# Token routing laid out as 784 consecutive tokens on each partition, with the zero fill and the second layer's weights placed elsewhere

## The chip, the core and the metric

The kernel runs on one core of one Trainium2 chip. Its engines are TensorE (PE, with PEld for its weight loads), VectorE (DVE), ScalarE (ACT) and GpSimd (POOL); SyncE (SP) issues most of the DMAs. Each engine takes its instructions in order and waits for the others on semaphores. The metric is the device time of one execution in microseconds. The time before is 16481.53 us, the median of three runs (16472.82 to 16503.21).

## What is computed

Two layers over x of shape 32 x 128 x 56 x 56, that is T = 100352 tokens of C = 128 channels. The first is a 7x7 depthwise convolution, a layer norm and a mixture of E = 8 experts with two picks for each token and a limit on each expert's tokens; the second is a convolution block with a Mamba scan over each image. The routing of the first layer is what matters here:

```python
logits = xf @ Wg + bg
topv, topi = jax.lax.top_k(logits, 2)
wts = jax.nn.softmax(topv, axis=-1)
order = jnp.argsort(-wts[:, 0])              # surest tokens first
cap = int(1.25 * T / E)                      # 15680 places for each expert
pos = cumsum(one_hot(topi[order]))           # place among the tokens of that expert
keep = pos < cap
buf[slot] = xf[order]                        # one row for each kept pick
y = gelu(buf @ W1 + b1) @ W2 + b2            # by expert
moe = sum over the two picks of y[slot] * weight
out = input + xf + layer_scale * moe
```

An expert that more tokens pick than it has places for keeps those of highest weight; where weights are equal, the earlier token goes first.

## The kernel before

The program is written as stages, one after the other. A scheduler gives each engine its order; it keeps close to the program's order, but it may take an instruction forward if its operands and its memory are ready. Memory is handed out in pools: the tiles of a closed pool make room for those of the next, and an instruction that writes into reused memory waits. Before the change a pool waits for all the tiles of the pool that lay there.

1. **Convolution** (L113 to L269). Images are taken in batches of four. `fill` loads an image into the single tile `xt` (L145), turns it on PE and copies it into `xc`. `conv` multiplies by Toeplitz tiles; in batch 0 these come from the raw taps (`raw`, L162, from `taps_d`, which the prologue makes from seven tap loads, L138, and one store, L139) and are kept in `toep_d`; later batches load them (L172). `norm` (16 for a batch) does the layer norm of seven columns of tokens, stores them to `res_d` (L213; `xa` has three buffers) and makes the logits; `top2` leaves the two picks and the difference of their logits in `picks` and `less`. The work of `norm` and `top2` for a batch is laid between the convolutions of the next, and for the last batch it follows the last convolution.
2. **Zero fill** (L272 to L274). The places of the experts' buffer `buf_d`, 125440 rows of 520 bytes, are written with zeros and the index T, from a constant tile of 112 rows, row by row, in 14 DMAs on SP. The tile is made at the start (L67 to L69), and the DMAs stand on SP's queue from 3.1 us on, among those of the convolution.
3. **Routing** (L277 to L442). Tokens lie as in the convolution, 112 on the partitions and 896 columns. `key` holds for each expert its tokens' weights. A search of 24 steps (L354 to L358) halves the interval for each expert's threshold: `count` counts the tokens over the bound (four experts on ACT with Sign, four on DVE), `totals` adds over the partitions on PE, and two small DVE instructions move the bounds of all eight experts. Then for each expert the places: masks of those over and at the threshold, on PE the counts of tokens before them, a scan over the columns, and the sums `sl`. At the end the places and the weights are turned on PE to 128 partitions (L431 to L442), giving `slots` and `gates`.
4. **Scatter** (L451 to L473). Blocks of 128 x 28 tokens are loaded to `xg` (L465, three buffers for each pick), and 1568 indirect DMAs on POOL (L469) write 128 rows each to their places.
5. **Experts** (L478 to L564). Blocks of 512 rows are loaded (`xb`, L552), turned and multiplied on PE, and added to `res_d` by 984 indirect DMAs on POOL (L518).
6. **Layer 1's weights** (L567 to L709). 28 loads on SP, among them six small columns that the scheduler takes forward into the routing, then some small work that makes `wk`, `wz`, `wo` and others from them.
7. **Layer 1** (L714 on). An order written by hand, `work`, over 224 chunks of 448 tokens. `fetch` loads `x1` and `yg` (the latter from `res_d`, L762), `moe_pe` (L770 to L772) adds them up on PE.

The DMAs of SP start in the order of its queue, and an issue is held up when what is ahead has not drained; the zero fill, the raw taps, `xt`, `toep`, `res_d`, `xg`, `xb` and the weights all use it.

Of the kernel before, what the change touches and what calls it, by code (L numbers as in the profile page):

```python
# [5 lines left out]
F32 = mybir.dt.float32  # L6
# [16 lines left out]
KF = FF // 128  # L23
GT = 4
# [19 lines left out]
def tile_kernel(tc: tile.TileContext, a: dict, out: bass.AP):  # L44
# [6 lines left out]
    QB = COLS // 128  # L51
    assert CAP % TT == 0
# [4 lines left out]
    with (  # L57
# [8 lines left out]

        zero = const.tile([TT, 1, RW], F32, name="zero")  # L67
        nc.gpsimd.memset(zero, 0.0)
        nc.gpsimd.memset(zero[:, :, C + 1].bitcast(I32), T)  # L69
# [26 lines left out]
        routed = tc.tile_pool(name="route", bufs=1)  # L96
# [175 lines left out]
        buf_t = buf_d[: E * CAP].rearrange("(k p) c -> p k c", p=TT)  # L272
        for k in range(0, E * CAP // TT, 80):
            nc.sync.dma_start(out=buf_t[:, k : k + 80, :], in_=zero.to_broadcast([TT, 80, RW]))  # L274


        with (  # L277
            tc.tile_pool(name="rt", bufs=1) as rt,
            tc.tile_pool(name="rs", bufs=2) as rs,
            tc.tile_pool(name="rp", bufs=2, space=PSUM) as rp,  # L280
        ):
            ones_tt = rt.tile([TT, TT], F32, name="ones_tt")
            nc.vector.memset(ones_tt, 1.0)
            before = rt.tile([TT, TT], F32, name="before")
            nc.gpsimd.affine_select(
                out=before, in_=ones_tt, compare_op=ALU.is_gt, fill=0.0, base=0,
                pattern=[[1, TT]], channel_multiplier=-1,
            )
            pb = rp.tile([TT, TT], F32, name="p_before", tag="tot")
            nc.tensor.matmul(pb, lhsT=before, rhs=perm, start=True, stop=True)  # L290
            half = rt.tile([TT, TT], F32, name="half")
            nc.vector.tensor_copy(half, pb)
            pb = rp.tile([TT, TT], F32, name="p_before", tag="tot")
            nc.tensor.matmul(pb, lhsT=half, rhs=perm, start=True, stop=True)
            nc.vector.tensor_copy(before, pb)
            ones_row = rt.tile([TT, COLS], F32, name="ones_row")
            nc.vector.memset(ones_row, 1.0)

            slots = [route.tile([128, QB, TT], I32, name=f"slot{k}") for k in range(2)]
            gates = [route.tile([128, QB, TT], F32, name=f"gate{k}") for k in range(2)]  # L300
            key = rt.tile([TT, E, COLS], F32, name="key")
            m = rt.tile([TT, COLS], F32, name="m")

            w0 = rt.tile([TT, COLS], F32, name="w0")
            w1 = rt.tile([TT, COLS], F32, name="w1")
            nc.scalar.activation(w1, less, AF.Exp)
            nc.vector.tensor_scalar_add(w0, w1, 1.0)
            nc.vector.reciprocal(w0, w0)
            nc.vector.tensor_tensor(w1, w1, w0, ALU.mult)

            nc.vector.tensor_scalar_max(m, w0, 0.5)
            for e in range(E):
                second = rs.tile([TT, COLS], F32, name="second")
                for k, t in enumerate((key[:, e, :], second)):
                    nc.vector.scalar_tensor_tensor(t, picks[k], float(E - e), m, ALU.is_equal, ALU.mult)
                nc.vector.scalar_tensor_tensor(key[:, e, :], key[:, e, :], -0.5, second, ALU.add, ALU.add)

            cnt = rt.tile([TT, E], F32, name="cnt")

            def totals():  # L320

                p = rp.tile([TT, E], F32, name="p_tot", tag="tot")
                nc.tensor.matmul(p, lhsT=ones_tt, rhs=cnt, start=True, stop=True)
                return p
# [4 lines left out]
            EV = E // 2  # L329
            thr = rt.tile([TT, E], F32, name="thr")  # L330
            cand = rt.tile([TT, E], F32, name="cand")
            odd = rt.tile([TT, E], F32, name="odd")
            step = rt.tile([TT, E], F32, name="step")
            need = rt.tile([TT, E], F32, name="need")
            nc.vector.memset(need[:, :EV], float(CAP))
            nc.vector.memset(need[:, EV:], float(2 * CAP - T))
            nc.vector.memset(thr, 0.0)

            def count(lim, op, shift):

                nc.vector.tensor_scalar(odd[:, EV:], lim[:, EV:], -(2.0**25), shift, ALU.mult, ALU.add)
                for e in range(EV, E):
                    sign = rs.tile([TT, COLS], F32, name="sign")
                    nc.scalar.activation(
                        sign, key[:, e, :], AF.Sign, bias=odd[:, e : e + 1], scale=2.0**25,
                        accum_out=cnt[:, e : e + 1],
                    )
                for e in range(EV):
                    junk = rs.tile([TT, COLS], F32, name="junk")
                    nc.vector.tensor_scalar(  # L350
                        junk, key[:, e, :], lim[:, e : e + 1], None, op, ALU.add, accum_out=cnt[:, e : e + 1]
                    )

            for b in range(1, 25):  # L354
                nc.vector.tensor_scalar_add(cand, thr, 2.0**-b)
                count(cand, ALU.is_ge, 1.0)
                nc.vector.tensor_tensor(step, totals(), need, ALU.is_ge)
                nc.vector.scalar_tensor_tensor(thr, step, 2.0**-b, thr, ALU.mult, ALU.add)  # L358


            count(thr, ALU.is_gt, -1.0)
            room = rt.tile([TT, E], F32, name="room")
            p = totals()
            nc.vector.tensor_scalar(room[:, :EV], p[:, :EV], -1.0, float(CAP), ALU.mult, ALU.add)
            nc.vector.tensor_scalar(room[:, EV:], p[:, EV:], -0.5, float(CAP - T // 2), ALU.mult, ALU.add)

            PB = min(448, COLS)
            NB = COLS // PB
            assert NB * PB == COLS and NB <= 2

            tots = [[rt.tile([TT, 1 + COLS], F32, name=f"tot{k}_{i}") for i in range(2)] for k in range(2)]
            for k in range(2):
                for i in range(2):
                    nc.vector.memset(tots[k][i][:, 0:1], 0.0)
            masks = [dict() for e in range(E)]

            def mask(e):

                for k, op in enumerate((ALU.is_gt, ALU.is_equal)):
                    t = masks[e][k] = rs.tile([TT, COLS], F32, name=f"mask{k}")
                    nc.vector.tensor_scalar(t, key[:, e, :], thr[:, e : e + 1], None, op)
                    pin = masks[e]["in", k] = rp.tile([TT, NB, 512], F32, name=f"p_in{k}", bufs=1)
                    pall = rp.tile([TT, NB, 512], F32, name="p_all", bufs=1)
                    for j in range(NB):
                        mj = t[:, j * PB : (j + 1) * PB]
                        nc.tensor.matmul(pall[:, j, :PB], lhsT=ones_tt, rhs=mj, start=True, stop=True)
                        nc.tensor.matmul(pin[:, j, :PB], lhsT=before, rhs=mj, start=True, stop=True)
                    nc.scalar.copy(  # L390
                        tots[k][e % 2][:, 1:].rearrange("p (j t) -> p j t", j=NB), pall[:, :, :PB]
                    )


            sl = [rt.tile([TT, COLS], F32, name=f"sl{k}") for k in range(2)]
            for k in range(2):
                nc.vector.memset(sl[k], 0.0)
            mask(0)
            for e in range(E):
                if e + 1 < E:  # L400
                    mask(e + 1)
                gt, eq = masks[e][0], masks[e][1]
                rk = []
                for k in range(2):
                    r = rs.tile([TT, COLS], F32, name=f"rk{k}")
                    nc.vector.tensor_tensor_scan(r, ones_row, tots[k][e % 2][:, :COLS], 0.0, ALU.mult, ALU.add)
                    rv = r.rearrange("p (j t) -> p j t", j=NB)
                    nc.vector.tensor_tensor(rv, masks[e]["in", k][:, :, :PB], rv, ALU.add)
                    rk.append(r)

                lim = room[:, e : e + 1]
                nc.vector.scalar_tensor_tensor(eq, rk[1], lim, eq, ALU.is_lt, ALU.mult)
                nc.vector.tensor_tensor(gt, gt, eq, ALU.add)
                nc.vector.scalar_tensor_tensor(rk[0], rk[1], lim, rk[0], ALU.min, ALU.add)
# [5 lines left out]
            for k in range(2):  # L420
                nc.vector.tensor_scalar_add(sl[k], sl[k], float(ZR))
            for k, w in enumerate((w0, w1)):
                nc.vector.scalar_tensor_tensor(w, sl[k], float(ZR), w, ALU.is_lt, ALU.mult)
# [784 lines left out]
```

## Time and profile before

| what | value |
|---|---|
| median of the runs | 16481.53 us |
| the profiled execution | 16440.87 us, span 16439.1 us |
| convolution, last logits | to 1664.94 us |
| routing, first indirect DMA of the scatter | to 2002.13 us |
| scatter, first load for the experts | to 3999.20 us |
| experts, last issue of an indirect DMA | to 5926.99 us |
| layer 1 | from there to the end |
| granted TensorE clock, mean | 0.905 |

The profile is of one execution. Times are from the span's start. Its page gives each engine's busy time, its share in 40 slices (a slice is 411 us, a digit is tenths), the groups of instructions and their releasers, and the DMA queues. A timeline row has the start, the length, the engine, the line in the code, the operation, what it writes and reads, and in brackets how long the engine stood before it and what ended that. A row of a queue (SPq) has the time that the issue took, not the transfer's.

### The profile page before, as it was taken

The numbers are of one execution on the slowest core, as the hardware profiler recorded it, in microseconds if no ns is written. First come the engines' busy times: TensorE is split into PE (matmuls) and PEld (weight loads), VectorE is DVE, ScalarE is ACT, GpSimd is POOL, SyncE is SP. The second block draws the span as 40 slices with busy tenths as digits, with TensorE's granted clock in tenths as the row PEclk, the third lists the DMA queues.
The fourth block names the chain that finished last, engine by engine and source line by source line (L and its number), as shares of the span: only waits on it lengthen the run. The fifth ranks groups of instructions, "written<-read, shape, count | busy, mean of one in ns | idle before, by whom it ended". The sixth has DMA issues, their size and how long they took to land. (4 is left out here: it accounts for less than half of the span.)

```text
span 16439.1 us, 246023 instructions
## 1 busy us (share of the span) xinstructions
PE 12744.6 (78%) x91548; PEld 6997.7 (43%) x91548; DVE 11159.9 (68%) x9974; ACT 10663.7 (65%) x20955; POOL 13614.8 (83%) x9017
## 2 busy tenths in 40 slices
PE   5997200002999989998898999999989899989998
PEld 4997100001777744444444444444444444444443
DVE  1564700000111149999999999999999999999999
ACT  3555300001444458888888888888888888888887
POOL 1434177777888879999999999999999999999999
PEclk8997555556999999999999999999999999999999
DMA  9879233333555545555555555555555555555555
GB/s 257 237 231 230 67 102 106 102 106 76 71 70 72 70 103 175 175 174 176 174 176 174 175 175 176 173 175 177 174 174 173 175 176 174 174 177 175 173 176 162
DMA packets 1360754, 2572.09 MB, mean 156 GB/s; under 512 B 139112, under 2 KB 801856, under 8 KB 1355456
## 3 DMA queue, kind: packets, MB, share of 16 engines
q1 hardware_dynamic: 1163072, 2361.89, 47.6%
q0 software_dynamic: 196480, 194.45, 6.9%
q8 instruction: 721, 11.81, 0.3%
q14 instruction: 481, 3.94, 0.1%
HBM read 2180.38 MB, written 375.43 MB: 155 GB/s over the span
## 5 line engine op out<-in xcount | busy, mean ns | idle before, releaser
L1053 POOL TENSOR_TENSOR db<-du,bb 128x896 f32<-128x896 f32 x3584 | 6856.5, 1938 | 17.6
L1059 ACT ACTIVATE da<-dt,aneg 128x449 f32<-128x449 f32 x7168 | 4577.8, 639 | 269.2 <-DVE prod L1074 86.5
L1068 DVE TENSOR_TENSOR_SCAN da<-da,db 128x898 f32<-128x898 f32 x2240 | 4523.6, 2019 | 1.9 <-ACT da L1059 1.5
L1013 PE MATMUL py<-prod,ident 64*64 64x448 f32 x28672 | 3100.0, 545 | 23.1 <-POOL prod L1074 17.5
L1068 DVE TENSOR_TENSOR_SCAN hs<-da,db 128x898 f32<-128x898 f32 x1344 | 2673.2, 2014 | 469.4 <-ACT db L1080 438.3
L1074 POOL TENSOR_TENSOR prod<-hs,cb 128x896 f32<-128x896 f32 x1344 | 2599.7, 1934 | 432.9 <-PE p_cvc L783 323.1
L1074 DVE TENSOR_TENSOR prod<-da,cb 128x896 f32<-128x896 f32 x2240 | 2446.0, 1092 | 217.3 <-issue 3.6
L560 ACT COPY xc<-ept 128x512 f32<-128x512 f32 (+1 forms) x248 | 144.1, 581 | 2905.2 <-DMA xb<-buf_d 2016.3
L469 POOL DMA_INDIRECT buf_d<-xg,slot x1568 | 1518.0, 968 | 486.2 <-issue 484.7
L518 POOL DMA_INDIRECT res_d<-ys,xb x984 | 1588.8, 1615 | 340.4 <-issue 275.7
L558 PE MATMUL ept<-ident,xb 128*128 128x128 f32 (+1 forms) x984 | 188.7, 274 | 2016.0 <-DMA xb<-buf_d 2016.0
L1013 PEld LDWEIGHTS py<-prod,ident 64*64 64x64 f32 x28672 | 1042.7, 132 | 1448.6 <-issue 1173.6
L868 PE MATMUL p_xm<-te,wk 128*128 128x448 f32 x3584 | 1415.8, 546 | 0.7 <-DVE te L852 0.6
L466 DVE COPY xg<-gate 128x28 f32<-128x28 f32 x56 | 12.1, 233 | 1776.2 <-DMA buf_d<-xg,slot 1776.1
L510 DVE TENSOR_TENSOR ys<-py,b2t 128x512 f32<-128x512 f32 (+2 forms) x256 | 170.8, 670 | 1460.5 <-PE py L504 1447.6
L504 PEld LDWEIGHTS py<-w2t,hh 128*128 128x128 f32 x7872 | 936.3, 191 | 175.7 <-issue 112.9
L504 PE MATMUL py<-w2t,hh 128*128 128x128 f32 x7872 | 985.0, 278 | 0.3
L558 PEld LDWEIGHTS ept<-ident,xb 128*128 128x128 f32 (+1 forms) x984 | 124.5, 143 | 2019.5 <-issue 2019.1
L180 PE MATMUL pc<-xc,toep 112*112 112x112 f32 (+1 forms) x8192 | 933.5, 270 | 49.0 <-ACT toep L169 45.9
L868 PEld LDWEIGHTS p_xm<-te,wk 128*128 128x128 f32 x3584 | 657.7, 189 | 731.4 <-issue 573.4
L210 POOL TENSOR_TENSOR xa<-xa,lng 112x896 f32<-112x896 f32 x128 | 267.5, 2090 | 771.3 <-ACT xa L207 711.9
L180 PEld LDWEIGHTS pc<-xc,toep 112*112 112x112 f32 x8192 | 878.6, 184 | 59.2 <-ACT toep L169 53.7
(244 smaller groups left out, 19714.4 us busy)
## 6 DMA issues: line engine op xcount, KB each, us to landing
bb<-bc_d SPq DMA_DIRECT2D x1792, 448.0 KB
cb<-bc_d SPq DMA_DIRECT2D x1792, 448.0 KB
toep<-toep_d SPq DMA_DIRECT2D x448, 392.0 KB
xg<-res_d SPq DMA_DIRECT2D x56, 1792.0 KB
buf_d<-zero SPq DMA_DIRECT2D x14, 4550.0 KB
xb<-buf_d SPq DMA_DIRECT2D x240, 260.0 KB
xt<-in_x SPq DMA_DIRECT2D x32, 1568.0 KB
res_d<-xa SPq DMA_DIRECT2D x128, 392.0 KB
```

The source lines that it names most:

```text
L180: nc.tensor.matmul(pc[:, c, :, lo:hi], lhsT=tp[c // 2][:, c % 2, 6 - 2 * o : 8 - 2 * o, :], rhs=s4[:, c, :, lo + o - 1 : hi + o - 1], star ...
L210: nc.gpsimd.tensor_tensor(xa, xa, lng.unsqueeze(1).to_broadcast([TT, w, C]), ALU.mult)
L469: apart(nc.gpsimd.indirect_dma_start(out=buf_d[:, :], out_offset=bass.IndirectOffsetOnAxis(ap=slots[k][:, q, p0 + j : p0 + j + 1], axis=0) ...
L504: nc.tensor.matmul(py[:n, j, :], lhsT=hh[:, k, j * 128 : j * 128 + n], rhs=w2t[:, k, :], start=k == 0, stop=k == KF - 1,)
L518: apart(nc.gpsimd.indirect_dma_start(out=res_d[:, :], out_offset=bass.IndirectOffsetOnAxis(ap=xb[:n, j, C + 1 : C + 2].bitcast(I32), axis= ...
L558: nc.tensor.transpose(pt[:, j * 128 : j * 128 + n], xb[:n, j, :C], ident[:n, :n])
L868: nc.tensor.matmul(p[:, :CH1], lhsT=s["wk"][:, k, hs], rhs=d["te"][:, k : k + CH1], start=k == 0, stop=k == DC - 1 and not first,)
L1013: nc.tensor.matmul(ps[r][h * HD : (h + 1) * HD, :CH1], lhsT=lhsT(rs, h), rhs=rhs[rs, h, :], start=start, stop=stop,)
L1053: nc.gpsimd.tensor_tensor(dbv[i][:, :, 1:], st[g]["du"], units[u].pop("bb"), ALU.mult)
L1059: nc.scalar.activation(da[:, h * W1 : (h + 1) * W1], st[g]["dt"][:, h, :], AF.Exp, scale=s["aneg"][:, h, i : i + 1])
L1068: nc.vector.tensor_tensor_scan(hs, da, dbs[i], 0.0, ALU.mult, ALU.add)
L1074: eng.tensor_tensor(w["prod"], w["hs"][:, :, 1:], w.pop("cb"), ALU.mult)
```

## The change

The routing is written anew, and two pieces of work are moved.

- **Layout.** `picks` and `less` are turned on PE first, to 128 partitions of PT = 784 consecutive tokens each. All of routing then has 128 x 784 elements, and the slots and gates come out as the scatter needs them. The scatter takes its blocks by the same order.
- **Search.** The eight experts are two halves of four. Each half has its own bounds and counts, and the steps of the halves are issued in turn. `need` is added by PE in the same sum, so that a step is two DVE instructions. Of each half, two experts are counted on ACT and two on DVE.
- **Places.** Running counts by scan along a partition, plus the counts of the partitions before it from PE. The sums over experts are made on PE with the identity.
- **Zero fill.** Its tile is 128 x 35 rows, in the pool of the routing, and each partition writes 35 consecutive rows (18200 bytes): 28 DMAs.
- **Weights of layer 1.** `weights` holds what stage 6 did; it is called in the scatter, after the block q = 3. Its tiles are in a pool of their own below those of the scatter and the experts.
- **Pools.** `route` lies at the other end of memory. The pools of routing, scatter, experts and layer 1 get `reuse_waits="tile"`: a tile waits only for those tiles in whose memory it lies.

```diff
-        zero = const.tile([TT, 1, RW], F32, name="zero")
-        nc.gpsimd.memset(zero, 0.0)
-        nc.gpsimd.memset(zero[:, :, C + 1].bitcast(I32), T)
...
-        routed = tc.tile_pool(name="route", bufs=1)
+        routed = tc.tile_pool(name="route", bufs=1, side="right")
...
-        buf_t = buf_d[: E * CAP].rearrange("(k p) c -> p k c", p=TT)
-        for k in range(0, E * CAP // TT, 80):
-            nc.sync.dma_start(out=buf_t[:, k : k + 80, :], in_=zero.to_broadcast([TT, 80, RW]))
...
-            tc.tile_pool(name="rt", bufs=1) as rt,
-            tc.tile_pool(name="rs", bufs=2) as rs,
+            tc.tile_pool(name="rt", bufs=1, reuse_waits="tile") as rt,
+            tc.tile_pool(name="rs", bufs=2, reuse_waits="tile") as rs,
...
+            zero = rt.tile([128, ZT, RW], F32, name="zero")
+            nc.gpsimd.memset(zero, 0.0)
+            nc.gpsimd.memset(zero[:, :, C + 1].bitcast(I32), T)
+            buf_t = buf_d[: E * CAP].rearrange("(p k) c -> p k c", p=128)
+            for k in range(0, E * CAP // 128, ZT):
+                nc.sync.dma_start(out=buf_t[:, k : k + ZT, :], in_=zero)
...
+            for q in range(QB):
+                p = rp.tile([128, 3, TT], F32, name="p_turn", tag="tot", bufs=3)
+                for k, v in enumerate((*picks, less)):
+                    nc.tensor.transpose(p[:, k, :], v.rearrange("p (j q) -> p j q", q=QB)[:, :, q], ident[:TT, :TT])
+                nc.scalar.copy(turned[:, :, q, :], p)
...
+            def keys(i):
+                v = E - i
+                z = rs.tile([128, PT], F32, name="junk")
+                nc.vector.scalar_tensor_tensor(z, both[0], float(-v), both[1], ALU.mult, ALU.add)
+                nc.vector.scalar_tensor_tensor(key[:, i, :], z, float(-v * v), m, ALU.is_equal, ALU.mult)
+                if i % HE >= 2:
+                    nc.scalar.activation(key[:, i, :], key[:, i, :], AF.Identity, bias=shift)
...
+            for b in range(1, 25):
+                for h in range(2):
+                    step = rs.tile([128, HE], F32, name=f"step{h}")
+                    nc.vector.tensor_scalar(step, total(cnts[h], need), 0.0, 2.0**-b, ALU.is_ge, ALU.mult)
+                    nc.vector.scalar_tensor_tensor(
+                        cands[h], step, -(2.0 ** -min(b + 1, 24)), cands[h], ALU.add, ALU.add
+                    )
+                    cnts[h] = count(h, ALU.is_ge if b < 24 else ALU.is_gt)
...
+            def scan(i):
+                nc.vector.tensor_tensor_scan(upto[:, i, :], ones, tie[:, i, :], 0.0, ALU.mult, ALU.add)
...
+            def chosen(i):
+                t = tie[:, i, :]
+                r = rs.tile([128, PT], F32, name="junk")
+                nc.vector.tensor_tensor(
+                    r.rearrange("j (r t) -> j r t", t=RUN), upto[:, i, :].rearrange("j (r t) -> j r t", t=RUN),
+                    over[:, i, :].unsqueeze(2).to_broadcast([128, PT // RUN, RUN]), ALU.is_gt,
+                )
+                nc.vector.tensor_tensor(r, r, t, ALU.mult)
+                nc.vector.scalar_tensor_tensor(
+                    t, key[:, i, :], cands[i // HE][:, i % HE : i % HE + 1], r, ALU.is_gt, ALU.add
+                )
+                scan(i)
+                return earlier(upto[:, i, PT - 1 : PT])
+
+            def places(i, p):
+                nc.vector.tensor_scalar_add(base[:, i : i + 1], p, float(i * CAP - 1 - ZR))
+                t = rs.tile([128, PT], F32, name="place")
+                nc.vector.scalar_tensor_tensor(t, upto[:, i, :], base[:, i : i + 1], tie[:, i, :], ALU.add, ALU.mult)
+                f = rs.tile([128, PT], F32, name="place0")
+                nc.vector.scalar_tensor_tensor(f, pick[0], float(E - i), t, ALU.is_equal, ALU.mult)
+                for v, to in zip((f, t), sums):
+                    for k in range(2):
+                        nc.tensor.matmul(
+                            to[:, k, : PT // 2], lhsT=ident, rhs=v[:, k * PT // 2 : (k + 1) * PT // 2],
+                            start=i == 0, stop=i == E - 1,
+                        )
...
+        w3pool = tc.tile_pool(name="w3", bufs=1)
+        w3p = w3pool.__enter__()
...
-            res_b = res_d[:T, :].rearrange("(q j p) c -> q j p c", j=128, p=TT)
+            res_b = res_d[:T, :].rearrange("(j q p) c -> q j p c", q=QB, p=TT)
...
+                if q == QB // 2:
+                    w3 = weights(w3p, w3t, p3t)
...
-            tc.tile_pool(name="ew", bufs=2) as ew,
-            tc.tile_pool(name="eb", bufs=3) as eb,
+            tc.tile_pool(name="ew", bufs=2, reuse_waits="tile") as ew,
+            tc.tile_pool(name="eb", bufs=3, reuse_waits="tile") as eb,
...
-            layer1(locals())
+            layer1(w3 | locals())
+        w3pool.__exit__(None, None, None)
```

## The prediction

> **What bounds the kernel now.** I read the slices of the page first, to find the stages, then the busy time by stage, then the timelines at each border. No engine bounds the whole program. Five stages follow one another, each with its own limit, and the change touches the first three and the two last borders. The slices:
>
> ```profile
> PE   5997200002999989998898999999989899989998
> DVE  1564700000111149999999999999999999999999
> POOL 1434177777888879999999999999999999999999
> DMA  9879233333555545555555555555555555555555
> ```
>
> The DMA digit is highest at the start and in the fourth slice, where the convolution begins and ends. The busy table (columns: stretch, length, then PE, PEld, DVE, ACT, POOL busy with counts, clock, DMA share, GB/s):
>
> ```profile
> 0.00:160.00 160.00, 25.36 (x119) 18.91 (x120) 0.43 (x12) 24.29 (x38) 7.21 (x17) 0.85 1.07 208
> 160.00:346.00 186.00, 132.97 (x1109) 121.29 (x1109) 19.75 (x32) 69.15 (x84) 30.99 (x59) 0.92 0.94 306
> 346.00:1501.00 1155.00, 1099.17 (x10243) 1066.20 (x10244) 656.12 (x2196) 669.72 (x1320) 468.24 (x224) 0.95 0.82 236
> 1501.00:1665.00 164.00, 69.34 (x340) 62.49 (x339) 69.87 (x283) 79.86 (x160) 66.38 (x32) 0.51 1.23 214
> 1665.00:2002.00 337.00, 91.44 (x210) 45.12 (x210) 297.83 (x505) 128.95 (x235) 3.84 (x5) 0.58 0.16 28
> 2002.00:3999.00 1997.00, 0.00 (x0) 0.00 (x0) 15.31 (x100) 0.00 (x0) 1518.03 (x1568) 0.50 0.33 103
> ```
>
> The convolution's middle is PE's (1099 of 1155 us). Its first 160 us and last 164 us belong to no engine, but to the DMA queue. Routing (337 us) is VectorE's. The scatter is GpSimd's: 1568 indirect DMAs, one each 1.273 us. The experts (to 5929) are PE's, 1899.75 of 1930 us. Layer 1 (10439 us from 6000) has VectorE busy 93%, GpSimd 95%; nothing in it changes. What holds the two ends of the convolution is seen in the timelines:
>
> ```profile
> 29.75 0.34 SPq L274 DMA_DIRECT2D buf_d<-zero  x1
> 31.39 18.48 SPq L139 DMA_DIRECT2D taps_d<-xt  x1
> ...
> 90.18 3.60 PE L150 MATMUL p_in<-ident,xt 128*112 128x128 f32 x16 [90.18 <-DMA xt<-in_x]
> ...
> 159.55 12.93 PE L180 MATMUL pc<-xc,toep 112*112 112x112 f32 x128 [0.49 <-ACT xc L152]
> ...
> 1652.25 3.89 ACT L207 ACTIVATE xa<-xc,nm,rs 112x128 f32<-112x128 f32 x7 [4.22 <-DMA res_d<-xa]
> ```
>
> The zero fill (L274, 14 DMAs of 4550 KB) shares SP's queue with the loads that the first matmul needs and the stores that free xa: 5 are issued by 140.5, one at 1334, 8 from 1491 to 1673. What stands behind one waits for it.
>
> **The change part by part.** The working is against the profiled span, 16439.1 us (16440.87 around it).
>
> *Zero fill out of the convolution, start.* Before, the taps land, xt lands (90.2), three more images follow, PE starts at 159.55. Without fills: seven tap loads issue from 4 to 7 us and land at about 13 (an estimate; the upper end is the 31.4 of the trace). The taps_d store takes 4 more, the first image 8.5 (96.27 to 104.92 for the second), each further one 15.9 (issues at 96.27 and 112.14), the last transposes 7.4 (152.16 to 159.55): 13 + 4 + 8.5 + 3 x 15.9 + 7.4 = 80.6, a gain of 79. The first 16 raw loads after that hold SP 30.40 us, the next 32 only 46.61, so 7 more go. The rest of batch 0 stays DMA-bound (0.94 share). **Gain 85**, ends 62 and 95.
>
> *The one at 1334.* From the 70-matmul run at the batch's border to PE's next long run: 37.4 us (1338.66 to 1376.07), against 20.8 at an earlier border (842.57 to 863.38), with some 2 us less matmul in between. **Gain 14**, ends 8 and 17.
>
> *Tail.* After the last conv matmul (1501) come a top2 and 16 norms. The first three norms start 6.1 and 4.0 us apart (1514.32, 1520.47, 1524.51), later ones wait for stores behind fills. ACT has 79.86/16 = 5.0 us in each. At 6.0 the last starts at 1514.3 + 90 = 1604 and ends 13 later, at 1617. **Gain 48**, ends 30 (7.1 a norm) and 62 (5.0). After this PE, which bounds the middle, is late next: batches stay 166 us.
>
> *Routing by 128 x 784 in two halves.* Before, 327 us from the last logits (1664.94) to the last gate. A step of the threshold search takes 5.80 us, because each step waits for the chain count, PE total, step, bound, count. All per-token instructions shrink from 896 to 784 elements; back to back they stand 1.00 us (two-tensor), 1.065 (count), 1.95 (scan) apart in the trace, so 0.88, 0.94 and 1.71. These are estimates by length. The sum:
> - last top2 13, 21 transposes of three planes (7 x 1.4 on a slow PE) 10, Exp, reciprocal (5.7 before, 5.0), m: 7; 16 key operations and the first counts, partly beside these: 17. Together 47.
> - 24 steps: VectorE has for each half step and bound 0.40, two counts 1.88, a gap of 0.1: 4.8 for both. ACT has 2 x (0.3 + 2 x 0.92) = 4.3. A half's own chain (step 0.4, odd 0.3, two signs 2.0, PE 0.6, hand-overs 0.2) is 3.5, shorter than 4.8, so the other half covers it: 24 x 4.8 = 115, was 139.
> - last totals and room 3; eight ties and scans 8 x 2.3 = 18; over 2; eight experts of chosen and places 4.4 + 1.9 = 6.3, 50 in all (was 8 x 14.49 = 116, read from the repeating masks); last sums and slots 8. PE's four 392-wide sums of an expert are hidden: two 448-wide matmuls took at most 1.8 us here.
>
> Total 243 with rounding 240. **Gain 87**, ends 60 and 105. The gates need no transposes at the end. The xg load still starts after it, about 10 us, as before.
>
> *The fill's new place.* It reuses memory of wg and bg, which the last norm reads, so it starts at the end of the convolution: memset of 4550 elements 4 us (3248 took 2.81), then 28 DMAs, 65.2 MB, ahead of the xg loads on SP, and the scatter waits for them. The trace has no store in 18 KB pieces. By the stretch 160 to 346, 306 GB/s: 213 us, with memset and landing 220, inside the 240. By its own old form, 520-byte rows at 214 GB/s: 305 + 6 = 311, 71 over. I take 306: long pieces are nearer to that stretch's 2 to 3.6 KB pieces than to 520 bytes. A rule speaks against it: the Trainium skill, DMA: Bandwidth & Descriptors, section Latency and other measured facts, gives 207 GB/s for a row pitch of 512 KiB and 103 at 4 MiB, where partitions run in lockstep. The fill's pitch is now 980 x 520 B = 509,600 B, 14 KiB short of 512 KiB. The same rule has the rate whole again 4 KiB off, and no run here shows pitch. By the row the fill costs 0, by 207 GB/s 315 + 6 - 240 = 81. **Cost 0**, ends 0 and 81.
>
> *Layer 1's weights into the scatter.* 22 loads join SP there (six more ran in the routing already), 13 us of issue (5929.5 to 5942.8), beside the xg loads (one each 35 us, three buffers deep); PE, ACT idle and VectorE 15 us busy in 1997. GpSimd gets nothing. Cost 0; without that cover some 13 us. The gain is at the end of the experts:
>
> ```profile
> 5925.56 1.43 POOL L518 DMA_INDIRECT res_d<-ys,xb  x1 [0.31 <-issue]
> 5929.52 0.35 SPq L576 DMA_DIRECT2D cv1t<-in_cv_wT  x1
> 5942.83 0.43 SPq L762 DMA_DIRECT2D yg<-res_d  x1
> 5951.32 0.55 PEld L770 LDWEIGHTS p_moe<-x,ident 128*128 128x128 f32 x2
> ```
>
> The yg load then goes at 5929.5 and lands 2.2 later; p_moe starts at about 5931.5: 20 off. Waits by tile instead of by pool let the experts' weights in before the scatter ends: the first xb issues at 3999.3, not 4002.0: 3 off. **Gain 23**, ends 12 and 26. Scatter and experts themselves keep their order of rows, hence their time.
>
> Sum: 85 + 14 + 48 + 87 + 23 = 257. 16439 - 257 = 16182 for a profiled span. The median of the runs, 16481.53, lies 40.7 above the profiled execution, so **16225**.
>
> **Rivals.**
> 1. *The fill becomes routing's bound.* For: DMA share is zero in the search now, and the fill's 220 us lie only 20 under the routing's 240. Against: 306 GB/s was reached with reads mixed in. At 214 GB/s: +71, 16295. Chance 0.17.
> 2. *The convolution gives nothing*, as the fill was hidden behind PE. For: PE busy 95% in the middle. Against: PE idle to 90 us and the waits on res_d. Only routing and the border gain, 110: 16371. Chance 0.06.
> 3. *The halves don't overlap* on the in-order queues: 2 x 3.5 = 7.0 a step, 24 x 2.2 = 53 more: 16278. Against: the program issues them in turn. Chance 0.05.
> 4. *Slower.* The fill falls to lockstep writes. It costs as soon as it outlasts 240 us and turns the sum when it takes 240 + 257 = 497, less 6 for memset and landing, below 133 GB/s. At the rule's 103 GB/s: 633 + 6 - 240 = 399 more, 16624. For: a pitch near 512 KiB. Against: even 520-byte rows made 214. Chance 0.02.
>
> That the fill would still run inside the convolution is part of rival 2, and unlikely: its tile lies in memory that the convolution's tiles hold to the end.
>
> **How the numbers follow.** Forecast 0.70, rivals 0.17, 0.06, 0.05, 0.02. The gains' ends, taken as independent, give about 30 us to each side of 16225, the runs themselves 16472 to 16503 about 15 more; its own range is 16175 to 16275. To leave out no more than 2 in 10 it has to reach over rival 1 and 3: 16150 to 16320. About 0.2% (33 us) is what a measurement can tell. All cases but rival 4 and a sliver of rival 2 are faster by far more: faster 0.96, same 0.02, slower 0.02.
>
> **What would show it.** First conv matmul near 80 us; last near 1400; last logits near 1518; DMA share high and the fill's last issue before the last slot; step period 4.8; first indirect DMA near 1770; 1.273 us spacing kept; p_moe 3 us after the last indirect DMA. Wrong if a wait on the fill stands ahead of the first xg load or scatter, if the first matmul stays near 160, or if the search's period is 5.8 or more.

## The result, and the profile after

The changed kernel takes **16209.54 us**, median of four runs (16201.56 to 16215.17), against 16486.53 for the kernel before beside it: a ratio of 0.9831, 95% interval 0.9814 to 0.9848, or 277 us less. The forecast was 16225. The profiled execution has a span of 16199.8 us. In nm_columns, norm_split, weights_late, tail_three and after_again below, the 1568 indirect DMAs of the scatter stood 1.386 us apart on average instead of 1.273, and executions of the kernel before beside them took 16665 to 16698 us (beside the first two, three of seven took 16471 to 16481), so these runs are read by their stages, and their totals are only compared among the last three, which ran side by side.

The slices of the page of the changed kernel:

```profile
PE   7996100006999989999999999899899999999988
...
DMA  8785433334555555555555555555555555555555
```

PE has 7 in the first slice, where it had 5. In the fourth the DMA digit is 5 instead of 9: the convolution ends in that slice without the fill among its stores. The busy table by stage shows where the transfers went (stretch, length, busy PE, PEld, DVE, ACT, POOL with counts, clock, DMA share, GB/s; the share adds up the times of all packets, so it can pass 1):

```profile
0.00:71.00 71.00, 24.80 (x123) 18.55 (x124) 1.08 (x16) 24.49 (x39) 7.02 (x15) 0.78 0.56 179
71.00:320.00 249.00, 206.96 (x1798) 193.20 (x1797) 84.61 (x284) 126.70 (x202) 72.46 (x79) 0.93 0.90 298
...
1380.00:1525.00 145.00, 69.72 (x338) 62.57 (x336) 75.15 (x282) 78.51 (x160) 66.39 (x32) 0.51 0.17 45
1525.00:1768.00 243.00, 88.28 (x301) 66.47 (x301) 220.36 (x437) 120.13 (x271) 7.28 (x7) 0.58 0.67 279
```

The DMA share before the first matmul fell from 1.07 to 0.56, in the tail from 1.23 to 0.17; in the routing it rose from 0.16 to 0.67. The timeline has the first conv matmul, the fill's new place with the first xg load behind it, and the border to layer 1:

```profile
70.20 2.02 PE L179 MATMUL pc<-xc,toep 112*112 112x112 f32 x17 [0.51 <-ACT xc L151]
...
1529.49 113.07 SPq L286 DMA_DIRECT2D buf_d<-zero  x28
1758.21 12.03 SPq L646 DMA_DIRECT2D xg<-res_d  x3
...
1768.64 1.10 POOL L650 DMA_INDIRECT buf_d<-xg,slot  x1 [9.62 <-DMA xg<-res_d]
...
5686.00 1.43 POOL L702 DMA_INDIRECT res_d<-ys,xb  x1 [0.30 <-issue]
...
5691.84 2.05 PE L818 MATMUL p_moe<-perm,yg 112*128 112x112 f32 x8 [23.23 <-DMA yg<-res_d]
```

The convolution starts at 70.2 instead of 159.55. The 28 DMAs of the fill follow the end of the convolution. The first xg load doesn't wait for them: the profile puts its wait down to `spare` (L467), the last reader of the memory that xg takes, which ended at 1758.15. p_moe follows the last indirect DMA by 5.8 us, not 27.5.

By stages, with two profiles of each kernel (the second ones are before_again and after_again below; us):

| stage | before | changed |
|---|---|---|
| to the first conv matmul | 159.6, 165.9 | 70.2, 69.9 |
| first to last conv matmul | 1341.5, 1344.0 | 1309.6, 1315.7 |
| tail, to the last logits | 163.8, 175.1 | 145.1, 145.1 |
| routing, to the first indirect DMA | 337.2, 337.3 | 243.7, 243.7 |
| last indirect DMA to p_moe | 27.5, 27.7 | 5.8, 6.0 |
| p_moe to the end | 10486.1, 10509.2 | 10508.0, 10521.9 |

The tail gave the least: 19 to 30 us where 48 were forecast. Layer 1 looks slower in the first pair. Both were followed up.

### The profile page after: what moved, and what is told of

Its sections match the earlier page's. It is cut to its first block, busy times and chain, and to the rows that moved or that the text cites. A ratio compares the mean times of both kernels' runs of the same rounds, so it can differ in the third digit from the quotient of the medians.

```text
span 16199.8 us, 246168 instructions
## 1 busy us (share of the span) xinstructions
PE 12759.5 (79%) x91637; PEld 7021.4 (43%) x91637; DVE 11083.8 (68%) x9909; ACT 10643.5 (66%) x20982; POOL 13611.7 (84%) x9017
## 5 line engine op out<-in xcount | busy, mean ns | idle before, releaser
L647 DVE COPY xg<-gate 128x28 f32<-128x28 f32 x56 | 11.7, 213 | 1746.4 <-DMA buf_d<-xg,slot 1746.4
L936 PE MATMUL p_z<-te,wz 128*128 128x448 f32 x896 | 522.3, 717 | 466.3 <-ACT xm L930 466.3
```

Of the source, the lines that this page charges most:

```text
L936: nc.tensor.matmul(p[:, :CH1], lhsT=s["wz"][:, h * 128 : (h + 1) * 128], rhs=d["te"][:, DC - 1 :], start=True, stop=True,)
```

## The experiments

**before_again**: the kernel before, unchanged.

> The kernel before, unchanged, for a second profile. The layer-1 stage took 10438 us in its first profile and 10458 in the changed kernel's. If that is what one execution differs from another, the second profile has 10450 or more; if the change makes layer 1 slower, it has 10438 again.

Measured from the first scan of layer 1 to the end: 10461.9 us, 10438.6 in its first profile. In all twelve profiles of kernels with the changed routing this stretch took 10444 to 10472. One execution differs from another by this much, so no cost of the change can be told there; one of some 10 us isn't excluded by two profiles of the kernel before. The span was 16482.3, near the median: the profile behind the prediction was of a short execution, 23 us of it in layer 1 and 20 before the routing.

**fill_back**: the changed kernel with the old fill.

```diff
-            zero = rt.tile([128, ZT, RW], F32, name="zero")
...
-            for k in range(0, E * CAP // 128, ZT):
-                nc.sync.dma_start(out=buf_t[:, k : k + ZT, :], in_=zero)
+        zero = const.tile([TT, 1, RW], F32, name="zero")
...
+        for k in range(0, E * CAP // TT, 80):
+            nc.sync.dma_start(out=buf_t[:, k : k + 80, :], in_=zero.to_broadcast([TT, 80, RW]))
```

> The changed kernel with the zero fill as it was before: 112-row constant tile, row by row, 14 DMAs taken forward on SP among the convolution's. Theory (the fill on SP's queue held up both ends of the convolution; the new place costs nothing): first conv matmul back from 70 to about 150-160, last logits from 1525 back to 1650-1665, the routing keeps its 244 us, so the time rises by 125 to 140 us over the changed kernel's 16210. Rival (the convolution got faster by the pools' waits by tile or by the other memory, the fill was hidden): last logits stay near 1525 and the time within 15 us of 16210.

Measured: 16366.55 us, 157 above the changed kernel; first conv matmul at 175.5, last logits at 1704.0, routing 237.3. SP's queue in its timeline:

```profile
35.48 0.34 SPq L276 DMA_DIRECT2D buf_d<-zero  x1
36.86 21.01 SPq L141 DMA_DIRECT2D taps_d<-xt  x1
```

The store of the taps, which the first matmul needs, holds the queue for 21 us behind a fill; the first image stands 19 us behind the next (67.53 to 87.01). So the convolution's gain is the fill's. The effect is above the expected 125 to 140 us, as every part of the convolution was longer than in the kernel before (the tail 180.3 us, against 163.8 and 175.1); why is not shown.

**fill_rows**: the new place, but rows of 520 bytes.

```diff
-            buf_t = buf_d[: E * CAP].rearrange("(p k) c -> p k c", p=128)
+            buf_t = buf_d[: E * CAP].rearrange("(k p) c -> p k c", p=128)
```

> The changed kernel with the fill in its new place, but row by row: each of the 28 DMAs writes 128 x 35 pieces of 520 bytes, the 35 of a partition lying 128 rows apart. Theory (the rate follows from the length of the pieces): 214 GB/s as in the kernel before, 65.2 MB in 305 us, from 1530 to 1835; the first indirect DMA waits for it, near 1840 instead of 1769, so 70 us slower than the changed kernel. Rival (the rate is high because nothing else moves then, 425 GB/s in the changed kernel): the fill still ends near 1685 and the time doesn't change.

Measured: 16341.69 us, 132 slower than the changed kernel, with the first indirect DMA at 1907.9. Its busy table:

```profile
1700.00:1800.00 100.00, 34.24 (x84) 17.42 (x84) 62.55 (x73) 0.81 (x1) 0.80 (x1) 0.67 1.26 182
```

The fill is alone on the queue here and still moves only 182 GB/s: 65.2 MB take 358 us. So the rate isn't high merely because nothing else moves: the shape of the fill sets it, and the expected 70 us were too few. The edit changes two things at once, the length of the pieces (18200 to 520 bytes) and the distance between a partition's pieces in DRAM (none to 128 rows); which of them counts was not tried apart. That it is 182 and not 214 is not explained; the earlier figure contained other transfers.

**fill_pitch**: a second fill behind the first, to a spare buffer, with 524288 bytes from partition to partition.

```diff
+            far_d = dram.tile([128, 131072], F32, name="far_d")
+            for k in range(E * CAP // 128 // ZT):
+                nc.sync.dma_start(out=far_d[:, k * ZT * RW : (k + 1) * ZT * RW], in_=zero.rearrange("p k c -> p (k c)"))
```

> The changed kernel with a second fill behind the first on SP: the same tile in the same 28 pieces of 18200 bytes, but into a spare DRAM buffer in which the partitions lie exactly 524288 bytes apart (in the real fill 509600). If a row pitch of 512 KiB halves the rate, these 28 run at some 207 GB/s and take 315 us behind the first's 153, so the xg loads start about 240 us late. If pitch doesn't matter here, they run at 425 GB/s as the first, 153 us, to about 1840, and the first xg load starts some 80 us late.

The busy table, while the second fill runs:

```profile
1800.00:1850.00 50.00, 0.00 (x0) 0.00 (x0) 0.00 (x0) 0.00 (x0) 0.00 (x0) 0.50 1.01 426
```

426 GB/s at a pitch of exactly 512 KiB, as in the real fill. The 207 of the expectation is the figure of the row that the prediction cites. The routing took 323.4 us, 79.7 more: the second 153 us minus the slack of the first, which ended near 1683, some 75 us before the first xg load. That is also the point from which a slower fill would have cost time.

**halves_apart**: the two halves of the search one after the other.

```diff
-            for b in range(1, 25):
-                for h in range(2):
+            for h in range(2):
+                for b in range(1, 25):
```

> The changed kernel with the loops of the search exchanged: 24 steps of the first half, then 24 of the second. Theory (each half's chain of step, odd, signs, totals is 3.5 us and is covered only by the other half): 48 x 3.5 = 168 us for the search instead of 118, less some 9 us of the first half's ties and scans that fit into the gaps of the second: 40 to 53 us slower. Rival (the gain of the search comes from the shorter rows and the fewer instructions alone): less than 15 us slower.

Measured: 16260.92 us, 51 above the changed kernel; the routing 288.6, 44.9 more. VectorE in the changed kernel, then here:

```profile
1604.20 0.16 DVE L383 TENSOR_SCALAR step<-p_tot 128x4 f32<-128x4 f32 x1
```

```profile
1603.34 0.16 DVE L383 TENSOR_SCALAR step<-p_tot 128x4 f32<-128x4 f32 x1 [0.90 <-PE p_tot L368]
...
1606.68 0.16 DVE L383 TENSOR_SCALAR step<-p_tot 128x4 f32<-128x4 f32 x1 [0.90 <-PE p_tot L368]
```

With both halves a step starts with no bracket, hence no wait; over the 48 steps these waits are 0.5 us. With one, VectorE stands 0.90 us before a step, for PE's totals, 40.0 us over the steps, and the period is 3.34: 48 x 3.34 = 160 us against 118. The halves do cover each other.

**weights_back** and **weights_late**: layer 1's weights after the experts again; in the second their pools are opened there too.

```diff
-                if q == QB // 2:
-                    w3 = weights(w3p, w3t, p3t)
...
+        with (
+            tc.tile_pool(name="w3t", bufs=1, reuse_waits="tile") as w3t,
+            tc.tile_pool(name="p3t", bufs=2, space=PSUM) as p3t,
+        ):
+            w3 = weights(w3p, w3t, p3t)
```

> The changed kernel with the work on layer 1's weights after the experts again, the pools otherwise as changed. Theory (only the border gains): from the last indirect DMA to the first p_moe with yg some 27 us instead of 5.8, so about 21 us slower, and the scatter and the experts keep their lengths. Rival (the 22 loads in the scatter cost something there, or the layer-1 stage is slower because of the move): the scatter becomes shorter or the layer-1 stage some 20 us shorter, and the time stays.

Measured: 16219.95 us, not told from the changed kernel; p_moe 6.1 us after the last indirect DMA. The expectation failed. SP's queue has the loads long before their place in the program:

```profile
1852.46 4.57 SPq L481 DMA_DIRECT2D cv1t<-in_cv_wT  x1
...
5627.75 0.58 SPq L481 DMA_DIRECT2D dw<-in_L_conv_dw_w  x1
```

```diff
-        w3pool = tc.tile_pool(name="w3", bufs=1)
-        w3p = w3pool.__enter__()
...
+        w3pool = tc.tile_pool(name="w3", bufs=1)
+        w3p = w3pool.__enter__()
         with (
-            tc.tile_pool(name="w3t", bufs=1, reuse_waits="tile") as w3t,
+            tc.tile_pool(name="w3t", bufs=1) as w3t,
```

> The changed kernel with the work on layer 1's weights after the experts, and with its pools opened only there and waiting for whole pools, as in the kernel before. In weights_back the call stood there too, but its tiles had memory of their own, the scheduler took their loads forward into the scatter and the experts, and p_moe came 6.1 us after the last indirect DMA. Theory (the border's gain comes from the memory of its own, not from the place of the call): now the loads wait for the last expert, p_moe comes 27 us after the last indirect DMA, and the time is about 21 us above the changed kernel's. Rival (the border gains by the tile waits of the layer-1 pools): 6 us again.

Measured: p_moe 28.0 us after the last indirect DMA, and 16428.8 us in all, 24 above after_again beside it. In its timeline the loads start 3.5 us after the experts' last add (5890.23):

```profile
5893.76 0.35 SPq L481 DMA_DIRECT2D cv1t<-in_cv_wT  x1
...
5918.27 1.88 PE L819 MATMUL p_moe<-perm,yg 112*128 112x112 f32 x8
```

So the 22 us of the border come from memory that the loads may use early; where the call stands made no difference in weights_back. Two things were changed at once from weights_back to weights_late, the place where the pools open and their waits by tile, and which of them holds the loads back is not shown.

The layout of the pools has a price at the other end, which was overlooked. In weights_late the routing took 238.0 us, 5.7 less than in the changed kernel. Its pools lie otherwise: the first xg load waits for a scan (`upto`, L403), not for `spare`, and is issued at 1767.33, 13.5 us before the first indirect DMA (1780.84) instead of 10.4, so that it has landed when the slots are ready. In fill_back, where the fill's tile is not in the routing's pool, xg is early too, and the routing took 237.3.

**The tail.** A norm makes `rs`, the square root of the variance and then its reciprocal, from that `nm`, minus the mean times rs, and with both the normalised tokens `xa`; `lg` are its logits. This is from the tail in the changed kernel's timeline, where they come in pairs:

```profile
1426.79 0.48 ACT L200 ACTIVATE rs<-mv,eps 112x7 f32<-112x7 f32 x2
...
1428.80 0.22 DVE L228 TENSOR_TENSOR lg<-p_lg,bg 112x56 f32<-112x56 f32 x1 [6.23 <-PE p_lg L224]
1428.93 0.26 DVE L201 RECIPROCAL rs<-rs 112x7 f32<-112x7 f32 x2
1429.12 2.07 POOL L210 TENSOR_TENSOR xa<-xa,lnb 112x896 f32<-112x896 f32 x1
1429.16 2.13 DVE L203 SCALAR_TENSOR_TENSOR nm<-mv,rs 112x7 f32<-112x7 f32 x2
...
1431.30 2.81 ACT L206 ACTIVATE xa<-xc,nm,rs 112x128 f32<-112x128 f32 x5 [4.03 <-POOL xa L210]
```

ACT stands 4.03 us, put down to POOL. But nm, which this ACT needs too, ended at 1431.29, as late. The square roots were done at 1427.27; the reciprocal stood behind the addition to lg, which waited for PE; then nm, whose shortest took 0.15 us, took 2.13 for two beside POOL's instruction on xa (L210, the addition of lnb). The pattern comes again after 16.0 us.

**nm_columns**: nm from seven one-column products.

```diff
-                nc.vector.scalar_tensor_tensor(nm, mv[:, :, 0], -1.0, rs, ALU.mult, ALU.mult)
+                for j in range(w):
+                    nc.vector.tensor_scalar(nm[:, j : j + 1], mv[:, j, 0:1], rs[:, j : j + 1], -1.0, ALU.mult, ALU.mult)
```

> The changed kernel with nm (L203) as seven one-column products instead of one instruction with two tensors from memory. Theory: in the tail that one instruction stands up to 2 us because GpSimd's multiplication of xa runs, and the ACT that makes the next xa waits for it, so that two norms take 16.0 us; with columns two norms take about 14, the tail gets 12 to 16 us shorter. Rival (the tail is set by xa's three buffers and GpSimd's 4.2 us for each norm): the pattern of 16.0 us stays.

```profile
1434.81 2.08 POOL L211 TENSOR_TENSOR xa<-xa,lnb 112x896 f32<-112x896 f32 x1
1434.86 1.79 DVE L204 TENSOR_SCALAR nm<-mv,rs 112x1 f32<-112x1 f32 x14
1435.16 2.27 ACT L207 ACTIVATE xa<-xc,nm,rs 112x128 f32<-112x128 f32 x4 [2.19 <-POOL xa L210]
```

ACT starts 0.3 us after the first column, while POOL's addition (L211) still runs; so neither that addition nor a buffer had held it. The tail took 137.9 us, 7.2 less, about half of what was expected: two norms take 15.0 us, as the reciprocal is still behind lg.

**norm_split**: the logits of a norm after the normalisation of the next, in all batches.

```diff
-                pl = plg.tile([TT, w, E], F32, name="p_lg")
+                xas[b, i, q] = xa
+
+            def logits(b, i, q):
+                w = NP // 4
+                xa = xas.pop((b, i, q))
+                pl = plg.tile([TT, w, E], F32, name="p_lg")
```

> The changed kernel with norm cut in two, the logits of one norm issued after the normalisation of the next. Theory: in the tail DVE's addition to lg stands ahead of the next reciprocal and nm and waits for PE, which keeps ACT idle; with the logits one norm later ACT is busy 5.0 us of each norm, the 16 norms take 5 to 6.5 us each instead of 8.0, the tail 25 to 45 us less. Rival (buffers or GpSimd set the pace): the tail stays within 10 us of its 145.

Measured: tail 126.7 us, 18.4 less, short of the expected 25 to 45, and first to last conv matmul 1369.1, some 50 more. That loss wasn't foreseen: the middle is bounded by PE, and with another order of the side work PE waits more, 122 us between 75 and 1378 against 88 in after_again.

**tail_three**: only the last batch in three pieces, with four buffers for rs and nm instead of two.

```diff
+            def last(b):
+                parts = [divmod(n, 4) for n in range(4 * NB0)]
+                for n in range(4 * NB0 + 3):
+                    for part, late in ((stats, 0), (scale, 2), (logits, 3)):
+                        if 0 <= n - late < 4 * NB0:
+                            part(b, *parts[n - late])
```

> The changed kernel with the norms of the last batch alone issued in three pieces: statistics and nm two norms ahead, the multiplications of xa, the logits one norm behind; the batches before keep their order, so the convolution keeps its last matmul near 1380 to 1390. Theory (in the tail the in-order queues of ACT and DVE hold the next nm behind the logits of the norm before and behind GpSimd's multiplications): a norm takes 5.0 to 5.5 us instead of 8.0, the tail 105 to 118 us instead of 145, the time 27 to 40 us below the changed kernel's. Rival (xa's three buffers and the stores to res_d set 7 to 8 us): within 10 us of it.

Measured: tail 104.8 us, as expected, but first to last conv matmul 1365.3, so that the total, 16418.2 us, is not below after_again's 16405.0 but 13 above it. What ACT's square roots waited for, in after_again and then in tail_three (idle us, times):

```profile
  DVE mv L198: 51.1, 8
```

```profile
  DVE mv L200: 83.7, 17
```

With four buffers the scheduler had put the square roots of three norms side by side, and ACT, in order, stood there in the batches between as well. PE waited with it: for ACT's copies of the logits' input (xc_lg) 38.5 us between 75 and 1378, against 11.7 in after_again. tail_alone tests this.

**after_again**: the changed kernel beside these.

> The changed kernel itself once more, on the chip of the two others, as their measure. Expected 16200 to 16225 us, a tail of 145 us, and a layer-1 stage anywhere from 10436 to 10467, since in seven profiles with the same layer 1 it lay there.

Measured: 16405.0 us, outside the expected range, as its scatter was 179 us longer than in the first profile and the experts 18; the kernel before beside it took 16685.12, a ratio of 0.9831 again. The tail was 145.1 us, as expected, and layer 1 took 10472, 5 above its range. Its stages stand in the table above.

**tail_alone**: four buffers for the last batch alone.

```diff
-                rs = cp.tile([TT, w], F32, name="rs", bufs=4)
+                rs = cp.tile([TT, w], F32, name=f"rs{tag}", bufs=bufs)
...
+                    if n < 4 * NB0:
+                        stats(b, *parts[n], "_l", 4)
```

> tail_three, but with the four buffers of rs and nm for the last batch alone; the batches before have two again. In tail_three the tail took 104.8 us instead of 145.1 as expected, and the convolution before it 1365 us instead of 1316, because with four buffers the square roots of three norms stood one behind the other on ACT (x3 in its order) at each batch's start. Theory: now the order of every engine up to the last convolution is that of the changed kernel, so the convolution takes 1310 to 1324 us again, the tail 103 to 107, and the sum of both is 40 us below the changed kernel's. Rival (the convolution's 50 us came from the memory or from the last batch's work): the convolution stays near 1365 and the sum is no lower than the changed kernel's.

Measured: first to last conv matmul 1317.7 us, tail 104.6, last logits at 1491.7 instead of 1524.9 and 1530.7. So the four buffers of the earlier batches had cost the convolution its 50 us. ACT in the tail:

```profile
1442.87 0.30 ACT L202 ACTIVATE rs_l<-mv,eps 112x7 f32<-112x7 f32 x1
1443.07 3.88 ACT L214 ACTIVATE xa<-xc,nm_l,rs_l 112x128 f32<-112x128 f32 x7
1446.86 0.86 ACT L236 COPY xc_lg<-p_xa 128x448 f32<-128x448 f32 x2
1447.61 0.30 ACT L202 ACTIVATE rs_l<-mv,eps 112x7 f32<-112x7 f32 x1
```

ACT is without a pause here, 4.7 us a norm; in the next it stands 0.74 for PE, 5.7. The time was 16168.58 us (16460.78 before beside it), ratio 0.9820, 0.9807 to 0.9834. The stages show 33 to 39 us, a little under the expected 40; by the ratios it isn't told from the changed kernel's 0.9831, whose interval overlaps.

## Why the prediction was right, point by point

The total was right within 16 us, and each gain was found where it was placed. It is a sum of terms of which most were a little low and one, the tail, much too high. These errors cancelled in part, so that the total came within 16 us is partly luck.

- *Zero fill out of the convolution, start* (85): the first conv matmul gained 89 to 96 instead of 79. The chain of the sum held, its estimates were long: the first image is issued at 11.9 us (17 in the sum), the fourth 44.9 later (47.7), the first matmul 13.5 after that (15.9). fill_back shows that the fill was the cause.
- *The one at 1334* (14) and the 7 us of raw loads: first to last conv matmul gained 26 to 34 between the four profiles of the table. It also varies between executions of this same part, 1307 to 1328 us over the profiles with the changed order, so how much of the 5 to 13 us more than 21 belongs to it stays open.
- *Tail* (48): the term that was mis-sized. **The stores' waits went, and the tail gained 19 to 30**, at or below the low end of 30. The pace of 6.0 us a norm was read from the first three norms, 6.1 and 4.0 apart. In steady state it is 8.0. The waits that come next were not asked for: the reciprocal behind lg, and nm behind POOL. In the tail before, nm's showed little, since ACT waited for stores at other times. The same line of the tail before and after (minimum/median/maximum ns):

```profile
L204 DVE SCALAR_TENSOR_TENSOR nm<-mv,rs x16: 149/166/2055, 1514.1 to 1635.7; 112x7 f32<-112x7 f32 x16
```

```profile
L203 DVE SCALAR_TENSOR_TENSOR nm<-mv,rs x16: 152/1552/2053, 1392.8 to 1509.2; 112x7 f32<-112x7 f32 x16
```

- A rule for nm's wait stood in the Trainium skill, SBUF — State Buffer, section SBUF: two separate sides: a VectorE instruction with two inputs in SBUF and a GpSimd instruction that reads SBUF share a pair of ports, and the later one waits for the whole of the other. The trace agrees: 98 of the changed kernel's 128 nm took over 0.25 us, up to 2.05, and each of these ended within 0.03 us of the end of an instruction of GpSimd on xa; of the one-column products 14 took 1.79 us beside one. In the kernel before 94 of 128 nm, most of them ahead of the tail, show the same. nm_columns shows the one wait, tail_alone both: with both off ACT's path a norm takes 4.7 to 5.7 us, and the upper end of this term (62) can be had.
- *Routing* (87): the way from the last logits to the first indirect DMA gained 93.5. Beginning 43.3 us (47), search with the last totals 119.5 (118), ties and scans 14.1 (20 with over), eight experts 50.6 (50). Ties of the first half fit in before the end of the search, which the sum hadn't counted. Rival 3 fell with halves_apart: its price, 53, was 44.9. What the shorter rows and the new places gave each was not tried apart.
- *The fill's new place* (0): right. It has 75 us of slack instead of 20, as the rate is 425 to 428 GB/s, not 306. The pitch row was misread: it is for copies between HBM tensors, and their full rate in the same row is 214 GB/s, so its 207 at 512 KiB says that such a pitch costs almost nothing there; it halves the rate only at 4 MiB, and gives the mechanism as an inference. No slowing is seen at 512 KiB in stores from SBUF either (426 GB/s); larger pitches weren't tried. Rival 1's mechanism is real, by fill_rows, and its price would have been 132, not 71.
- *Layer 1's weights into the scatter* and the border (23): 22 at p_moe, and 2.8 at the experts' first xb load, which follows the last issue of the scatter by 2.4 us instead of 5.2. The size was right, the reason half: memory that is free early makes the gain, not the place of the call, and in this layout some 6 us are lost again at the first xg load, as weights_late and fill_back show. The scatter kept its spacing of 1.273 us.
- The median above the profiled execution (40.7): right to add; the second profile of the kernel before was at 16482.3.

## What to carry to other kernels

When a stall goes, read the pace behind it from a stretch without the stall or work out each in-order queue for it, and don't extrapolate from the first pieces, which find every queue empty. Where a wait names an engine, look for a small instruction that ends at the same moment and that the waiting one needs as well. Large fills and loads without a reader nearby belong where the DMA queues are idle, in pieces that lie together in DRAM and are as long as the memory allows, and work that is to come forward needs memory that is free then.

## What was not expected of the hardware

- The fill of 18200-byte pieces reaches 425 to 428 GB/s, close to the 436 that the Trainium skill (SBUF — State Buffer, section SBUF: two separate sides) gives for the DMA ports together; the same bytes in 520-byte rows 128 rows apart, alone on the queue, 178 to 182.
- A VectorE instruction of 112x7 elements with two inputs in SBUF took between 0.14 and 2.05 us; all that took over 0.25 ended within 0.03 us of an instruction of GpSimd.
- Indirect DMAs of 128 rows stood 1.273 us apart on average in nine of the fourteen profiles and 1.386 in the other five, with the same instructions: 178 us over the scatter. They aren't all slower. In after_again 1287 of the 1567 distances stay under 1.4 us (median 1.273), and 280 are longer, up to 2.8. From the fifth block on, 206 of these lie at the same nine places of each block's 56, and nm_columns and tail_three show the same places. What makes the difference was not found.
